# A GRU's first two steps: input products without Winograd sums, loads in order of use, ternary weights spread over VectorE

## The chip, the cores and the metric

The kernel runs on one core of a Trainium2 chip. The metric is device time in microseconds (us); for a kernel it is the median of several runs. TensorE (PE) multiplies, VectorE (DVE) and ScalarE (ACT) work on elements and read the products from PSUM, GpSimd (POOL) works on elements in SBUF and issues some DMAs, and SyncE (SP) issues most DMAs.

## The reference

Two blocks, each with a residual sum, on x of 128 sequences, 64 steps and 512 features, all in float32. Only the first concerns this change: a GRU over the 64 steps whose states go through a linear layer with ternary weights.

```python
def cell(h, x):
    gi = x @ W_ih + b_ih
    gh = h @ W_hh + b_hh
    i_r, i_z, i_n = jnp.split(gi, 3, axis=-1)
    h_r, h_z, h_n = jnp.split(gh, 3, axis=-1)
    r = jax.nn.sigmoid(i_r + h_r)
    z = jax.nn.sigmoid(i_z + h_z)
    n = jnp.tanh(i_n + r * h_n)
    h_new = (1.0 - z) * n + z * h
    return (h_new, h_new)
...
scale = jnp.mean(jnp.abs(weight))
w_t = jnp.clip(jnp.round(weight / (scale + EPS)), -1.0, 1.0)
w_ste = weight + jax.lax.stop_gradient(w_t * scale - weight)
return jnp.einsum('bsi,oi->bso', x, w_ste) + bias
```

The second block is a causal convolution over time, a mixture of 64 experts and a shared expert; the change leaves it as it is.

## The kernel before

The batch of 128 fills the partitions. A step t needs the input gates gi (x_t times W_ih, 512 by 1536) and the hidden gates (h times W_hh). The recurrence in h is serial: the hidden gates of step t are twelve 128x512 matmuls (L502), then come r, n, z and the new h on DVE and ACT (L509 to L523), then four transposes of h (L393) and a copy on ACT (L399).

The input gates don't depend on h, so they are made ahead and fill PE while the elementwise work of a step runs. They are made for two steps at a time: the pair of steps forms a 2 by 2 block matrix with the halves of the 512 features, W_ih of one gate a second one with the halves of its rows and columns. The two are multiplied by Winograd's form of Strassen's method: seven block products instead of eight, against sums of blocks. One product is two 128x256 matmuls (L338); the trace shows each float32 matmul as two passes, so a product is an entry "x4". `prepare(c)` makes the weight sums t1, t2, t4 and w12 of gate c on DVE (L287 to L292), and adds b_hh to b_ih where they can be added (L294). `pair_operands(t)` makes the sums of x: on POOL, for the first pair on DVE (L308 to L311). `Chunk.product(n)` makes product n and takes the results from PSUM on DVE, with the bias already in the chain (p1, u2, u3; L353 to L367).

`input_gates()` is a generator that gives one product at each `next`; the gates are taken in the order r, n, z, that is c = 0, 2, 1. Ahead of step 0 there are 24 products (20 of the first pair, which is all but its last, and four of the second pair in which that last one stands), and then 11 or 10 in each step: enough for a pair in two steps. In step 0's place in the order also lie the ternary weights: the load of wfT into xc0, the sum of its absolute values (L457, L460), a small matmul over the partitions (L462), the scale and the two bounds (L463 to L465), and for each of four parts of the weights two DVE instructions that make the signs `sgn` (L470, L471). The feed-forward product of step t - 1 (L417) is made in step t; its scale and residual are added on DVE (L428), with the bias fb added to x's rows on POOL ahead of it (L413).

The framework's scheduler orders each engine's instructions and sets the waits; `tc.issue_after(i)` puts what is made under it behind instruction i. Each tile pool has a number of buffers; a tile waits until the buffer's last reader is done. The PSUM tiles psx, psy, psw and psz have one buffer each.

The loads of the start go through SP's queue in program order: xp of the first pair, wih0 in two halves, biases, wih2, wih1, biases, h, xp of the second pair, whh0, whh2, whh1, fb, cb, rows of zeros, x's rows, wfT. From the ninth on, a DMA's issue waits until the eighth before it has landed.

Of the kernel before, what the change touches and what calls it, by code (L numbers as in the profile page):

```python
# [8 lines left out]
F32 = mybir.dt.float32  # L9
# [5 lines left out]
ALU = mybir.AluOpType  # L15
AX = mybir.AxisListType
# [3 lines left out]
P = 128  # L20
B = 128
T = 64
D = 512
KD = D // P
# [10 lines left out]
EPS = 1e-10  # L35
# [7 lines left out]
def adaln_ffn_kernel(  # L43
# [22 lines left out]
    nc = tc.nc  # L66
# [32 lines left out]
    def load_rows(dst, src):  # L99

        return nc.sync.dma_start(out=dst, in_=src.rearrange("(k p) n -> p k n", p=P))
# [98 lines left out]
    with (  # L200
# [11 lines left out]
        def load_pair(t, queue=nc.gpsimd):  # L212
            xp = xpp.tile([P, 2, KD, B], F32, name="xp")
            queue.dma_start(out=xp, in_=xT[t : t + 2].rearrange("t p k b -> p t k b"))
            xps[t] = xp
# [4 lines left out]
            (nc.sync if t < 3 else nc.gpsimd).dma_start(out=xn, in_=x[:, t, :])  # L220
            xns[t] = xn

        load_pair(0, nc.sync)
        h = el0.tile([P, D], F32, name="h")

        whh = [w0.tile([P, KD, D], F32, name=f"whh{c}") for c in range(3)]
# [12 lines left out]
        wi = wi_.enter_context(tc.tile_pool(name="wi", bufs=1))  # L239

        bi = wi.tile([P, 3 * D], F32, name="bi")
        wih = [wi.tile([P, KD, D], F32, name=f"wih{c}") for c in range(3)]

        xc0 = xcs[0].rearrange("p b e -> p (b e)")
        cols = [slice(c * D, (c + 1) * D) for c in range(3)]
# [1 line left out]
        def repeated(dst, row):  # L247
            nc.sync.dma_start(out=dst, in_=row.partition_broadcast(P))

        for h_ in range(2):
            half_ = slice(h_ * HD, (h_ + 1) * HD)
            load_rows(wih[0][:, h_ * HK : (h_ + 1) * HK], w_ih[half_, cols[0]])
        bh = {}
        for c in (0, 2, 1):
            if c:
                load_rows(wih[c], w_ih[:, cols[c]])
            repeated(bi[:, cols[c]], b_ih[cols[c]])
            if c != 2:  # L260
                bh[c] = el0.tile([P, D], F32, name="r")
                repeated(bh[c], b_hh[cols[c]])
        nc.sync.dma_start(out=h, in_=cond)
        load_pair(2, nc.sync)
        for c in (0, 2, 1):
            load_rows(whh[c], w_hh[:, cols[c]])
            if c == 0:
                repeated(bhn, b_hh[cols[2]])
        repeated(fb, fbias)
        repeated(cb, cbias)  # L270
        nc.gpsimd.memset(zrow, 0.0)
# [2 lines left out]

        nc.vector.memset(ones, 1.0)

        wsum = {}

        def prepare(c):

            w = wih[c]
            w11, w12 = w[:, :HK, :HD], w[:, :HK, HD:]
            w21, w22 = w[:, HK:, :HD], w[:, HK:, HD:]
            t1 = wi.tile([P, HK, HD], F32, name=f"t1{c}")
            nc.vector.tensor_sub(t1, w12, w11)  # L287
            t2 = wi.tile([P, HK, HD], F32, name=f"t2{c}")
            nc.vector.tensor_sub(t2, w22, t1)  # L289
            nc.vector.tensor_sub(w12, w22, w12)  # L290
            t4 = wi.tile([P, HK, HD], F32, name=f"t4{c}")
            nc.vector.tensor_sub(t4, w21, t2)  # L292
            if c in bh:
                nc.vector.tensor_add(bi[:, cols[c]], bi[:, cols[c]], bh[c])  # L294
            wsum[c] = {1: w11, 2: w21, 3: w22, 4: t4, 5: t1, 6: t2, 7: w12}

        gis, last = {}, []
        made = []

        def pair_operands(t):  # L300

            xp = xps.pop(t)
            x11, x12 = xp[:, 0, :HK], xp[:, 0, HK:]
            x21, x22 = xp[:, 1, :HK], xp[:, 1, HK:]
            s = xpp.tile([P, 3, HK, B], F32, name="xs")
            s1, s2, s4 = s[:, 0], s[:, 1], s[:, 2]
            engine = nc.gpsimd if t else nc.vector
            engine.tensor_add(s1, x21, x22)  # L308
            engine.tensor_sub(s2, s1, x11)
            engine.tensor_sub(x21, x11, x21)  # L310
            engine.tensor_sub(s4, x12, s2)  # L311
            return {1: x11, 2: x12, 3: s4, 4: x22, 5: s1, 6: s2, 7: x21}
# [56 lines left out]
        def input_gates():  # L369


            prev = None
            for t in range(0, T, 2):
                ops = pair_operands(t)
                for c in (0, 2, 1):
                    if t == 0:
                        prepare(c)
                    cur = Chunk(t, c, ops)
                    for n in (1, 6, 7, 3, 2, 4, 5):
                        which = prev if n == 3 else cur  # L380
                        if which:

                            with tc.issue_after(made[-1].ins) if t == 0 and made else nullcontext():
                                which.product(n)
                            yield
                    prev = cur
            prev.product(3)
            yield
# [7 lines left out]
        def transposed(src):  # L396
            ps = turned_up(src)
            hT = el0.tile([P, KD, B], F32, name="hT")
            nc.scalar.copy(hT, ps)  # L399
            return hT  # L400
# [6 lines left out]
            nc.vector.tensor_sub(lo, hT, hi)  # L407
            return hi, lo

        def ffn(t, pieces):  # L410

            xn = xns.pop(t)
            nc.gpsimd.tensor_add(xn, xn, fb)  # L413
            ps = ps_f.tile([P, D], F32, name="psf")
            for i, piece in enumerate(pieces):
                for k in range(KD):
                    nc.tensor.matmul(  # L417
                        ps,
                        piece[:, k, :],
                        sgn[:, k, :],  # L420
                        start=(i == 0 and k == 0),
                        stop=(i == 1 and k == KD - 1),
                    )
            if t < T - TAIL:
                x1 = io0.tile([P, D], F32, name="x1")
            else:
                x1 = last[0][:, t - (T - TAIL)]
            nc.vector.scalar_tensor_tensor(x1, ps, scale, xn, ALU.mult, ALU.add)  # L428
            if t < T - TAIL:
                nc.sync.dma_start(  # L430
                    out=x1c[:, T - 1 - t, :, :].rearrange("q b e -> b q e"),
                    in_=x1.rearrange("b (q e) -> b q e", e=DS),
                )
            if t == T - 1 - TAIL:
                for sl in range(2):
                    load_steps(sl, slice(0, LAST))
                for sl in range(2, NCB):
                    load_piece(sl)

            (nc.gpsimd if t >= T - TAIL else nc.sync).dma_start(out=out_t[t], in_=x1)  # L440
            if t == T - 1 - LAST:
                for sl in range(2):
                    load_toeplitz(sl)
                    load_steps(sl, slice(LAST, T))
# [3 lines left out]
        for _ in range(24):  # L448
            next(stream)
        hT = transposed(h)  # L450

        wf = xc0[:, : KD * D].rearrange("p (k o) -> p k o", k=KD)
        load_rows(wf, wfT)
        wfl = wf.rearrange("p k o -> p (k o)")
        nc.vector.tensor_reduce(  # L457
            part, wfl.rearrange("p (a c) -> p a c", a=T), AX.X, ALU.add, apply_absolute_value=True
        )
        nc.vector.tensor_reduce(total, part, AX.X, ALU.add)  # L460
        ps_s = ps_f.tile([P, D], F32, name="psf")
        nc.tensor.matmul(ps_s[:, 0:1], ones, total, start=True, stop=True)  # L462
        nc.vector.tensor_scalar(scale, ps_s[:, 0:1], 1.0 / (D * D), None, ALU.mult)  # L463
        nc.vector.tensor_scalar(half, scale, EPS, 0.5, ALU.add, ALU.mult)
        nc.vector.tensor_scalar(nhalf, half, -1.0, None, ALU.mult)  # L465


        for k in range(KD):
            neg = el0.tile([P, D], F32, name="r")
            nc.vector.tensor_scalar(neg, wf[:, k, :], nhalf, None, ALU.is_lt)  # L470
            nc.vector.scalar_tensor_tensor(sgn[:, k, :], wf[:, k, :], half, neg, ALU.is_gt, ALU.subtract)  # L471

        for t in range(T):
            if t + 1 < T:
# [31 lines left out]
            ps_r, ps_n, ps_z = ps_g  # L506

            r = el0.tile([P, D], F32, name="r")
            nc.vector.tensor_add(r, ps_r, gis.pop((t, 0)))  # L509
            nc.scalar.activation(r, r, AF.Sigmoid)  # L510
            n = el0.tile([P, D], F32, name="n")
            nc.vector.tensor_add(n, ps_n, bhn)  # L512
            nc.vector.tensor_mul(n, n, r)
# [9 lines left out]
            nc.vector.tensor_add(h_new, h_new, n)  # L523

            if t > 0:
                ffn(t - 1, pieces)
            for _ in range(11 - t % 2):
                next(stream, None)
            h = h_new
            if t < T - 1:  # L530
                hT = transposed(h)
# [231 lines left out]
    class Down:  # L763
# [37 lines left out]
        def block(self, name):  # L801

            if name == "v":
                self.accs["v"] = ps_y.tile([P, D], F32, name="y")[:, :QT]
            j, half_ = self.places[name]
            nc.tensor.matmul(
                self.accs[name],
                self.aT[:, full - 1, self.steps[j]],
                swd[:, full - 1, half_ * HD : (half_ + 1) * HD],
                start=(name == "v"),  # L810
                stop=False,
                skip_group_check=name != "v",
            )
# [707 lines left out]
```

## Time and profile before

| | us |
|---|---|
| median of 3 runs | 2654.07 |
| lowest and highest | 2651.58, 2656.09 |
| profiled execution | 2653.43 |
| its span | 2651.7 |
| first product (PE) | 6.24 |
| transposes of the first h (PE) | 32.07 |
| first hidden gates (PE) | 34.67 |
| wfT there, first reduce (DVE) | 36.55 |
| transposes of the new h of step 0 (PE) | 56.00 |

The times of the lower part are starts in the trace, counted from the start of the span. An entry of the timeline gives start, duration, engine, line, operation, output and inputs, shape and number of instructions; in brackets stands the engine's idle time before it and what ended it. A duration is that of the instruction from start to end; instructions of one engine overlap a little, so the distance from start to start is what one costs in a row of them.

### The profile page before, as it was taken

Reading aid. Unit: us, or ns where it says so; the run is one execution under the profiler, and the core shown is the slowest. Engines: PE = TensorE matmul, PEld = TensorE weight load, DVE = VectorE, ACT = ScalarE, POOL = GpSimd, SP = SyncE. Lnnn points to the kernel's source line nnn. Section 1 sums busy time; section 2 is a strip of 40 time slices with the busy share of each in tenths; the row PEclk is TensorE's granted clock in tenths of the full one; section 3 lists DMA queues with packets and bytes.
Section 4 is the critical chain, followed back from the end, with each engine's and each line's share of the span. In section 5 each row is a group of like instructions: output and inputs, shape, how many; then the busy total and the mean of one; then the engine's idle time right before and its main releaser. Section 6 shows DMA issues by size and latency. Waiting matters only on the chain.

```text
span 2651.7 us, 31084 instructions
## 1 busy us (share of the span) xinstructions
PE 2630.1 (99%) x11959; PEld 1818.1 (69%) x11959; DVE 1411.0 (53%) x3116; ACT 422.9 (16%) x779; POOL 458.6 (17%) x519
## 2 busy tenths in 40 slices
PE   8999999999999999999999999999999999999999
PEld 5666666666666666666668767888877666666667
DVE  6555555555555555555557755666674333434344
ACT  1111111111111111111110222222321111111111
POOL 2111121111111111111113100000002222222210
PEclk9999999999999999999999999999999999999999
DMA  5323232323322222322228921222256999998952
GB/s 195 70 56 61 53 63 55 67 56 62 61 49 52 44 52 44 76 44 52 44 56 279 337 52 22 43 64 64 76 157 180 286 314 285 292 328 261 303 176 48
DMA packets 475540, 323.33 MB, mean 122 GB/s; under 512 B 328960, under 2 KB 395136, under 8 KB 473216
## 3 DMA queue, kind: packets, MB, share of 16 engines
q1 hardware_dynamic: 446800, 248.18, 33.6%
q0 software_dynamic: 28592, 73.16, 11.3%
q8 instruction: 95, 1.56, 0.2%
q14 instruction: 53, 0.43, 0.0%
HBM read 235.01 MB, written 92.55 MB: 124 GB/s over the span
## 4 chain that ended last, share of the span: by engine, by line
PE 98%; DVE 1%; DMA 0%; issue 0%; ACT 0%; SPq 0%; DVEq 0%
PE psgh L502 25%; PE psz L695 7%; PE psw L695 7%; PE psx L695 7%; PE psw L338 6%; PE psz L338 6%; PE psx L338 6%; PE psf L417 4%; PE y L695 4%; PE py L1410 3%; PE psy L338 3%; PE pg L1384 3%; PE pu L1384 3%; PE y L870 2%; PE psc L182 2%; PE lg L1018 1%
## 5 line engine op out<-in xcount | busy, mean ns | idle before, releaser
L502 PE MATMUL psgh<-whh,hT 128*128 128x512 f32 x1536 | 674.7, 595 | 0.7 <-ACT hT L399 0.7
L502 PEld LDWEIGHTS psgh<-whh,hT 128*128 128x128 f32 x1536 | 286.6, 190 | 350.2 <-issue 336.3
L338 PE MATMUL psx<-wih,xp 128*128 128x256 f32 x768 | 198.7, 381 | 6.3 <-DMA wih<-in_w_ih_dram 6.2
L220 POOL DMA_DIRECT2D xn<-in_x_dram x61 | 34.0, 557 | 843.8 <-DVE x L428 832.2
L338 PEld LDWEIGHTS psx<-wih,xp 128*128 128x128 f32 x768 | 143.8, 191 | 25.9 <-issue 6.2
L512 DVE TENSOR_TENSOR n<-psgh,bhn 128x512 f32<-128x512 f32 x64 | 44.3, 692 | 175.6 <-PE psgh L502 175.6
L1393 DVE SCALAR_TENSOR_TENSOR a<-a,rw,pu 128x352 f32<-128x352 f32 x32 | 18.6, 581 | 220.4 <-PE pu L1384 220.4
L399 ACT COPY hT<-psf 128x512 f32<-128x512 f32 x64 | 37.5, 586 | 584.8 <-PE psf L393 584.8
L509 DVE TENSOR_TENSOR r<-psgh,gi 128x512 f32<-128x512 f32 x64 | 44.3, 691 | 139.8 <-PE psgh L502 139.8
L413 POOL TENSOR_TENSOR xn<-xn,fb 128x512 f32<-128x512 f32 x64 | 80.8, 1264 | 145.2 <-DMA xn<-in_x_dram 145.2
L972 POOL DMA_DIRECT2D out_dram<-hid x32 | 27.6, 1000 | 450.9 <-issue 332.9
L338 PE MATMUL psz<-wih,xs 128*128 128x256 f32 x384 | 98.7, 379 | 1.8 <-DVE gi L361 1.8
L338 PE MATMUL psy<-t,xs 128*128 128x256 f32 x384 | 99.9, 383 | 0.4 <-DVE t L289 0.4
L338 PE MATMUL psw<-wih,xp 128*128 128x256 f32 x384 | 99.4, 381 | 0.0
L338 PE MATMUL psw<-t,xp 128*128 128x256 f32 x384 | 98.8, 380 | 0.2 <-DVE u L359 0.2
L338 PE MATMUL psz<-t,xs 128*128 128x256 f32 x384 | 98.7, 379 | 0.0
L417 PE MATMUL psf<-sgn,hhi 128*128 128x512 f32 x256 | 95.4, 494 | 0.3 <-DVE hlo L407 0.3
L1410 PE MATMUL py<-wd,aeT 128*64 128x512 f32 (+1 forms) x384 | 89.5, 601 | 0.0
L353 DVE TENSOR_TENSOR p<-psx,bi 128x512 f32<-128x512 f32 x96 | 66.4, 692 | 37.6 <-PE psx L338 37.3
L515 ACT ACTIVATE n<-n 128x512 f32<-128x512 f32 x64 | 40.3, 629 | 274.0 <-DVE n L514 274.0
L695 PE MATMUL psx<-xr,swg 128*128 128x256 f32 x320 | 83.3, 383 | 0.0
L695 PE MATMUL psx<-hid,swg 128*128 128x256 f32 x320 | 82.4, 380 | 0.0
(311 smaller groups left out, 4711.6 us busy)
## 6 DMA issues: line engine op xcount, KB each, us to landing
wg<-in_w_gate_dram SPq DMA_DIRECT2D x64, 704.0 KB
wu<-in_w_up_dram SPq DMA_DIRECT2D x64, 704.0 KB
wd<-in_w_down_dram SPq DMA_DIRECT2D x64, 512.0 KB
x1c<-x SPq DMA_DIRECT2D x62, 256.0 KB
out_dram<-x SPq DMA_DIRECT2D x62, 256.0 KB
xn<-in_x_dram POOLq DMA_DIRECT2D x61, 256.0 KB, 4.1
xp<-in_xT_dram POOLq DMA_DIRECT2D x30, 512.0 KB, 5.0
xc<-x1c SPq DMA_DIRECT2D x28, 512.0 KB
```

The lines of the kernel that those rows point to most:

```text
L182: i = nc.tensor.matmul(ps[rows, j].rearrange("p h (u t) -> p h u t", u=2), xcs[sl % NCB][:, rows, g * 4 + j], tzs[sl % NCB][:, :, :, g * 4 ...
L338: i = nc.tensor.matmul(ps, self.ops[n][:, k, :], self.ws[n][:, k, :], start=(first and k == 0), stop=(k == HK - 1), skip_group_check=not f ...
L353: add(self.p1, both, b)
L413: nc.gpsimd.tensor_add(xn, xn, fb)
L417: nc.tensor.matmul(ps, piece[:, k, :], sgn[:, k, :], start=(i == 0 and k == 0), stop=(i == 1 and k == KD - 1),)
L502: nc.tensor.matmul(ps, hT[:, k, :], whh[c][:, k, :], start=(k == 0), stop=(k == KD - 1))
L509: nc.vector.tensor_add(r, ps_r, gis.pop((t, 0)))
L512: nc.vector.tensor_add(n, ps_n, bhn)
L695: i = nc.tensor.matmul(ps.rearrange("p (j b) -> p j b", b=P) if len(r.shape) == 3 else ps, lhs(k), r, start=(first and k == 0), stop=(k == ...
L870: nc.tensor.matmul(gu.rearrange("p (j b) -> p j b", b=P), swr[:, k].rearrange("p w n -> p (w n)"), rows[:, k], start=(k == 0), stop=(k == ...
L1384: nc.tensor.matmul(acc[halves[j]], self.xeT[:, k, halves[j]], self.ws[j][which][:, k, :], start=(k == 0), stop=(k == KD - 1),)
L1410: nc.tensor.matmul(py[halves[j]], self.aeT[:n, c, halves[j]], self.ws[j][2][:n, c, :], start=(c == 0), stop=(c == len(ech) - 1),)
```

## The change

- **First pair.** Steps 0 and 1 are no longer made by Winograd's form. `first_products(c, xp)` makes the eight plain block products of each gate, in an order in which each block of W_ih serves both steps one after the other, and ACT copies each finished 128x256 sum from PSUM into gi. This makes 24 products for the pair instead of 21. The biases are added to these gi later, on DVE (`first_biases`).
- **Sums.** `prepare` no longer comes ahead of each gate's products. Its DVE instructions and those of `first_biases` are chained by `in_order`, each behind the one before. `pair_operands` always uses POOL; the first pair has none.
- **Loads.** wih0 becomes four tiles of one block each, wih2 and wih1 two tiles of two blocks. SP's queue is in order of use: half of x's step 0, block (0,0), x's step 1, block (0,1), the other half of step 0, blocks (1,0) and (1,1), wih2, wih1, h, xp of the second pair, then biases and whh, and wfT right behind whh1, ahead of fb, cb and x's rows.
- **PE's start.** Seven 128x128 matmuls on the tile of ones, which nobody reads, precede the first product.
- **Ternary weights.** `ternary()` is a generator. The sum of absolute values becomes four instructions, each behind step 0's r on DVE; the scale follows; the four pairs of sign instructions come between the products of step 0, and what is left behind step 1's r. The temporary takes z's buffers instead of r's.
- **Feed-forward bias.** For t < 3, fb is added to x's rows on DVE, behind the r of the step, instead of on POOL.
- **Ahead of step 0**, after the transposes of h are put in, three products more are taken from the stream (27 in all).

```diff
-        load_pair(0, nc.sync)
+        xps[0] = xpp.tile([P, 2, KD, B], F32, name="xp")
...
-        for h_ in range(2):
-            half_ = slice(h_ * HD, (h_ + 1) * HD)
-            load_rows(wih[0][:, h_ * HK : (h_ + 1) * HK], w_ih[half_, cols[0]])
+        nc.sync.dma_start(out=xps[0][:, 0, :HK], in_=xT[0, :, :HK])
+        load_block(0, 0)
+        nc.sync.dma_start(out=xps[0][:, 1], in_=xT[1])
+        load_block(0, 1)
+        nc.sync.dma_start(out=xps[0][:, 0, HK:], in_=xT[0, :, HK:])
+        for n in range(2):
+            load_block(1, n)
+        for c in (2, 1):
+            for k in range(2):
+                load_half(c, k)
+        nc.sync.dma_start(out=h, in_=cond)
+        load_pair(2, nc.sync)
         bh = {}
         for c in (0, 2, 1):
-            if c:
-                load_rows(wih[c], w_ih[:, cols[c]])
             repeated(bi[:, cols[c]], b_ih[cols[c]])
             if c != 2:
                 bh[c] = el0.tile([P, D], F32, name="r")
                 repeated(bh[c], b_hh[cols[c]])
-        nc.sync.dma_start(out=h, in_=cond)
-        load_pair(2, nc.sync)
...
+        load_rows(whh[1], w_hh[:, cols[1]])
+        wf = xc0[:, : KD * D].rearrange("p (k o) -> p k o", k=KD)
+        load_rows(wf, wfT)
...
+        ps = ps_f.tile([P, D], F32, name="psf")
+        for _ in range(7):
+            nc.tensor.matmul(ps[:, :P], ones, ones, start=True, stop=True)
...
+        def first_biases(t):
+            for c in (0, 2, 1):
+                b = bi[:, cols[c]]
+                if t == 0 and c in bh:
+                    in_order(nc.vector.tensor_add, b, b, bh[c])
+                in_order(nc.vector.tensor_add, gis[t, c], gis[t, c], b)
+
+        def first_products(c, xp):
+            for t in range(2):
+                gis[t, c] = gip.tile([P, 2, HD], F32, name="gi").rearrange("p h d -> p (h d)")
+            accs = {}
+            for k in range(2):
+                for n in range(2):
+                    for t in range(2):
...
+                        for j in range(HK):
+                            i = nc.tensor.matmul(
+                                accs[t, n],
+                                xp[:, t, k * HK + j, :],
+                                block(c, k, n)[:, j, :],
+                                start=(k == 0 and j == 0),
+                                stop=(k == 1 and j == HK - 1),
+                            )
+                        made.append(i)
+                        if k == 1:
+                            nc.scalar.copy(gis[t, c][:, n * HD : (n + 1) * HD], accs[t, n])
+                        yield
...
-            for t in range(0, T, 2):
+            xp = xps.pop(0)
+            for c in (0, 2, 1):
+                for _ in first_products(c, xp):
+                    yield
+                if c == 0:
+                    prepare(0)
+            prepare(2)
+            first_biases(0)
+            prepare(1)
+            first_biases(1)
+            for t in range(2, T, 2):
...
-            nc.gpsimd.tensor_add(xn, xn, fb)
+            if t < 3:
+                with tc.issue_after(i.ins):
+                    nc.vector.tensor_add(xn, xn, fb)
+            else:
+                nc.gpsimd.tensor_add(xn, xn, fb)
...
+        for _ in range(3):
+            next(stream)
+        def ternary():
+            for k in range(KD):
+                with tc.issue_after(chain[-1].ins):
+                    nc.vector.tensor_reduce(
...
+            for k in range(KD):
+                yield
+                neg = el0.tile([P, D], F32, name="z")
+                nc.vector.tensor_scalar(neg, wf[:, k, :], nhalf, None, ALU.is_lt)
+                nc.vector.scalar_tensor_tensor(sgn[:, k, :], wf[:, k, :], half, neg, ALU.is_gt, ALU.subtract)
...
-            for _ in range(11 - t % 2):
+            for j in range(11 - t % 2):
                 next(stream, None)
+                if t == 0 and j in (0, 4, 8):
+                    next(signs)
```

## The prediction

> **What bounds the kernel now.** I read the page first (busy shares, then the chain that ended last), then busy time by stretches, then the timeline of the first 60 us. The page's busy line and its chain line:
>
> ```profile
> PE 2630.1 (99%) x11959; PEld 1818.1 (69%) x11959; DVE 1411.0 (53%) x3116; ACT 422.9 (16%) x779; POOL 458.6 (17%) x519
> ...
> PE 98%; DVE 1%; DMA 0%; issue 0%; ACT 0%; SPq 0%; DVEq 0%
> ```
>
> TensorE (PE) is the bound nearly everywhere, so the time is the PE's work plus the places where it stood still. Busy time by stretches says where those are (columns: stretch, its length, then busy us and instructions of each engine, clock, DMA share, GB/s):
>
> ```profile
> 0.00:60.00 60.00, 51.33 (x189) 35.89 (x190) 41.42 (x78) 6.22 (x8) 16.66 (x25) 1.00 0.62 215
> 60.00:800.00 740.00, 740.00 (x2655) 488.09 (x2654) 402.68 (x697) 105.66 (x171) 128.04 (x153) 1.00 0.30 58
> ```
>
> From 60 to 800 us PE has no gap at all; in the first 60 us it lacks 8.7 us. The change touches that start alone; the instructions of the rest stand in the same order, so whatever is won or lost there shifts all the rest by as much. The timeline, PE and DVE (start, length, engine, line, operands, count, idle before and who ended it):
>
> ```profile
> 6.24 2.04 PE L338 MATMUL psx<-wih,xp 128*128 128x256 f32 x4 [6.24 <-DMA wih<-in_w_ih_dram]
> 8.63 2.07 PE L338 MATMUL psy<-t,xs 128*128 128x256 f32 x4 [0.35 <-DVE t L289]
> 10.50 1.91 PE L338 MATMUL psw<-wih,xp 128*128 128x256 f32 x4
> 12.44 1.30 PE L338 MATMUL psx<-wih,xp 128*128 128x256 f32 x4
> ...
> 15.60 1.03 PE L338 MATMUL psx<-wih,xp 128*128 128x256 f32 x4
> 16.46 1.03 PE L338 MATMUL psy<-t,xs 128*128 128x256 f32 x4
> ```
>
> ```profile
> 36.55 2.29 DVE L457 TENSOR_REDUCE part<-xc 128x64 f32<-128x2048 f32 x1 [1.69 <-DMA xc<-in_wfT_dram]
> ...
> 44.94 1.41 DVE L471 SCALAR_TENSOR_TENSOR sgn<-xc,half,r 128x512 fp32r<-128x512 f32 x2
> ...
> 47.05 1.41 DVE L471 SCALAR_TENSOR_TENSOR sgn<-xc,half,r 128x512 fp32r<-128x512 f32 x2
> ...
> 48.38 0.68 DVE L509 TENSOR_TENSOR r<-psgh,gi 128x512 f32<-128x512 f32 x1
> ...
> 50.14 1.10 PE L338 MATMUL psz<-wih,xs 128*128 128x256 f32 x4 [1.76 <-DVE gi L361]
> ...
> 56.00 0.60 PE L393 MATMUL psf<-ident,h 128*128 128x128 f32 x4
> ```
>
> One block product (x4) starts every 0.865 us once warm (15.60, 16.46, 17.32), but the first three start about 2 us apart. The first waits until 6.24 for one megabyte of loads. Later the ternary work (the reduce waits for its weights, then eight sign instructions) sits on DVE ahead of r of step 0, which could have started near 38.4 (3.71 us after the gate products began at 34.67, as in step 1: 57.30 to 61.01) and starts at 48.38; PE then stands for 1.76 us at 50.14 and in pieces until 52.98.
>
> I take 56.00 as the mark: the transposes of h at the end of step 0. Work before it: 36 products x 0.865 = 31.14, transposes 0.44, gate products with the scale's small matmul 10.52 (34.67 to 45.19): 42.10. Elapsed from 6.24: 49.76. **Lost 7.66**: 4.17 in the first six products (6.24 to 15.60 against 6 x 0.865), 0.90 until 34.67, 2.59 from 45.19 to 56.00.
>
> **The Trainium skill.** "TensorE: Matmul & The Clock Gate", section "Part 1: The HAM clock gate", says that the array runs at half clock until a free-running window of about 3.4 us has been busy, so 3.4 to 6.8 us after the first matmul. The trace agrees in kind: products start 1.87 us apart while cold, and the fast rhythm begins near 12.4, 6.2 us after the first (with one gap of 0.35 in it). The same page's table of properties calls VectorE's queue strict FIFO: a waiting instruction holds all behind it, as L457 does above. "DMA: Bandwidth & Descriptors", section "Anatomy of one DMA", gives a fixed cost of some 2 us for a DMA of GpSimd's path; here, on SP's queue, the first load (0.5 MB) is issued at 0.81, and 3.25 us later, at 4.06, its reader starts. Its section "Why small descriptors are slow" counts 3 extra cycles a packet; for the 1 KB rows of the new blocks against 2 KB I estimate from it 35/32 against 67/64, some 4% more time. No run here shows that yet.
>
> **The change part by part.**
>
> *Earlier start.* Before, the first product needs 1.05 MB (xp and half of wih0). Now it needs 0.39 MB: half of x's first step and one block. In the trace data begins to move at about 2.0 us and flows at 296 GB/s in the stretch 2 to 4; 0.39 MB are in by 3.3, 3.5 with the smaller rows, and with 0.3 to 0.7 us to the semaphore (xp: 3.75 worked out, 4.06 seen) the product may start at 3.9 to 4.3. The seven matmuls on ones start at about 1.15 (the memset ends at 1.08); each is two passes of half the columns of L338's, so at the cold rate (1.73/8 = 0.215 a pass) they end near 4.15. Start: 4.2 instead of 6.24, **-2.04**. They cost nothing more, since PE would wait for the data; if the data came sooner they would hold it back by up to 0.3. The following loads keep ahead: 1.57 MB landed at 7.89 before and now serves eight products, which last until about 12.3.
>
> *Cold clock.* If PE is busy from 1.15, the clock should rise between 4.6 and 8.0; 6.2 us after the first, as before, gives 7.3. Half the time from 4.2 to there is lost: 0.2 to 1.9, I take **1.2**.
>
> *No sums before the first products.* The Winograd sums (L287 to L294) and the bias chain leave the path; each finished 128x256 sum is taken from PSUM by one ScalarE copy, 12 in all. The nearest row is a 128x512 ACT copy of 0.59, so about 0.4 each, against four products (3.46 us) between uses of a PSUM tile: hidden, ScalarE was idle until 32.7. Instead **three more products**: 24 for the first pair instead of 21, 3 x 0.865 = **+2.60**.
>
> *Order on DVE.* Sums for the later pairs and the adding of biases run behind. The last gate's bias add waits for ScalarE's copy after product 23 (25.9 by my schedule); behind it in the queue stand four sums, three adds, p1, u2, u3, eleven at 0.60 to 0.65, so free at 32.6, and r is due at 29.2 + 3.7 = 32.9. It fits with 0.3 to spare, while PE does the gate products (29.2 to 39.5) and needs none of it.
>
> *Ternary weights.* wfT moves ahead of the constants and of x's rows on SP's queue: 10.2 MB up to and with it. The stretches of the trace (6.1 MB by 20 us, 10.0 by 30) put it at 30.5 to 31.8, and 0.7 to 2.5 more to the semaphore. The four reduces (2.29/4 = 0.57 each) follow r at 33.5 and end at 35.9; n is due at 36.3. The four pairs of sign instructions (0.40 + 0.66) are spread over the eleven products of step 0. I laid DVE's queue out one by one: z 40.2, the new h 44.0, p1 44.6, then with two sign instructions between, u3 at 46.7, which PE's n = 4 product of that chunk wants at 46.6. So DVE is close to the limit there; **0.3** for gaps, 0 to 1.5 as bounds. The last signs end near 53.5; the first feed-forward product comes near 61. The add of fb to xn for three steps, now on DVE behind r (0.69 each), lies in an idle stretch: DVE waited 2.74 for psgh before n in step 1. POOL loses 3 x 1.24 us that nobody waited for. whh's loads, behind 5.0 MB, land by about 20.5, 25.2 and 28.6, needed at 29.2, 32.6 and 36.1.
>
> *Sum.* Start 4.2 + cold 1.2 + 24 products 20.76 + transposes 0.44 + 3 products 2.60 + gate products 10.3 + scale 0.24 + 11 products 9.52 + gaps 0.3 = 49.56 at the mark, against 56.00: -6.44. At the mark the new kernel has 637 of its 675 products to come, the old one 636 of 672: +0.87. Together **-5.6 us**. Cross-check: -2.04 - (7.66 - 1.5) + 2.60 = -5.6. On the profiled execution (2653.43; span 2651.7 and 1.7 around it) this is 2647.8; the median of the runs is 0.64 higher, so 2648.5.
>
> **Rivals.**
> 1. *Part of the gain is lost to late data or a late DVE.* If the start gets data at 300 GB/s less a quarter, or u3 and its followers are 1.5 us late, or the gate stays cold until near 9, the gain falls to about -2.5: 2651.6. For it: DVE's slack of 0.3 in two places, and DVE instructions that took 1.04 and 1.21 instead of 0.68 beside POOL (22.43, 23.40). Against: POOL's adds for pair 2 come before 20 us now, when DVE has room.
> 2. *Slower: wfT is late and takes the place of the old wait.* All of n, z, h and the evacuations stand behind the reduces in DVE's queue. PE loses what wfT lands after 33.9 (reduces 2.3, then the 10.4 from n to u3, against 46.6). Break-even is a landing at about 39.5; at 46 the loss is 12.1, the sum +6.5: 2660.6. For it: it landed at 36.55 before, 12.0 after its issue at 24.52. Against: it is now issued near 18 to 19, once the eighth load before it has landed, with 1.1 MB less ahead; the same flight gives 31.
>
> **How the numbers follow.** A difference under 0.2% (5.3 us) can hardly be told from none. Forecast 0.78, with its own range -7.8 to -3.6 (start 0.4, cold 0.7 to 1.0, gaps up to 1.2 either way); rival 1 0.15; rival 2 0.07. The forecast lies just beyond the bound; nearly three quarters of its chance (0.57) I put past it, because the page's clock window more often ends earlier than I took and the gaps may be none; the other 0.21 and rival 1 are "same", 0.36; rival 2 is "slower", 0.07. The range takes in rival 1: 2645.5 to 2652.8.
>
> **What would show it.** First product near 4.2, products 0.865 apart from about 7; step 0's gate products at about 29 instead of 34.67; no idle before them; reduces straight behind r without a wait for DMA; the transposes at about 49.6; from there every time about 5.6 earlier. Wrong would be: a reduce that waits for in_wfT, a PE gap over 1 us between 40 and 50, cold products past 9 us, or a different pace after 60 us.

## The result and the profile after

| | before | after |
|---|---|---|
| median of 18 runs, us | 2653.81 | 2648.81 |
| lowest and highest | 2651.58, 2656.09 | 2646.83, 2652.55 |
| profiled execution | 2653.43 | 2647.67 |
| its span | 2651.7 | 2645.9 |
| first product (PE) | 6.24 | 4.28 |
| first h's transposes (PE) | 32.07 | 26.28 |
| transposes of step 0's new h (PE) | 56.00 | 49.33 |
| transposes of step 1's new h (PE) | 76.43 | 70.62 |

The ratio of the times is 0.9981, with a 95% interval of 0.9975 to 0.9988: 5.0 us less (3.2 to 6.6). In the two profiled executions the span is 5.8 us shorter. The forecast was 2648.5. At 0.19% the gain stands just inside the 0.2% under which, the prediction says, a difference can hardly be told from none; its interval lies clear of zero.

First the page of the changed kernel, its busy line and its chain line:

```profile
PE 2631.8 (99%) x11985; PEld 1823.5 (69%) x11985; DVE 1402.9 (53%) x3103; ACT 427.4 (16%) x791; POOL 453.2 (17%) x516
...
PE 98%; DVE 1%; DMA 1%; issue 0%; SPq 0%; ACT 0%; DVEq 0%
```

PE is busy 1.7 us longer and still the bound: it makes three more products and the matmuls on ones, while fewer products run at half speed. Busy time by stretches of the changed kernel (stretch, length, busy us and instructions of PE, PEld, DVE, ACT and POOL, clock, DMA share, GB/s):

```profile
0.00:60.00 60.00, 58.87 (x226) 43.40 (x227) 37.66 (x66) 11.36 (x21) 13.59 (x22) 1.00 0.61 215
60.00:800.00 740.00, 740.00 (x2657) 488.69 (x2656) 402.69 (x701) 105.87 (x171) 127.05 (x153) 1.00 0.30 58
```

In the first 60 us PE is busy 58.87 us, against 51.33 before; from 60 to 800 us it is busy throughout, as before. The clock column reads 1.00 although the first products run at half speed; that is seen from the distances between their starts. The timeline of the changed kernel's start, on PE:

```profile
1.13 3.36 PE L303 MATMUL psf<-ones 128*128 128x128 f32 x14 [1.13 <-DVE ones L299]
4.28 1.97 PE L345 MATMUL psx<-wih,xp 128*128 128x256 f32 x4
6.05 1.41 PE L345 MATMUL psw<-wih,xp 128*128 128x256 f32 x4
7.29 1.03 PE L345 MATMUL psy<-wih,xp 128*128 128x256 f32 x4
8.15 1.03 PE L345 MATMUL psz<-wih,xp 128*128 128x256 f32 x4
...
26.28 0.60 PE L461 MATMUL psf<-ident,h 128*128 128x128 f32 x4
...
29.31 10.46 PE L583 MATMUL psgh<-whh,hT 128*128 128x512 f32 x24
...
46.74 1.03 PE L399 MATMUL psw<-t,xp 128*128 128x256 f32 x4
...
49.33 0.60 PE L461 MATMUL psf<-ident,h 128*128 128x128 f32 x4
```

No entry from the first product on has a bracket, so PE waits for nothing that the profile shows. The distances from start to start of the first products are 1.77, 1.24 and 0.86: the clock is released (goes from half to full speed) about 6.8 us after the start of the span, in the middle of the second product. The same stretch on DVE:

```profile
6.94 0.69 DVE L323 TENSOR_TENSOR t<-wih,wih 128x512 f32<-128x512 f32 x1 [5.87 <-DMA wih<-in_w_ih_dram]
...
32.95 0.69 DVE L590 TENSOR_TENSOR r<-psgh,gi 128x512 f32<-128x512 f32 x1
33.87 2.47 DVE L532 TENSOR_REDUCE part<-xc 128x16 f32<-128x512 f32 x4 [0.23 <-DMA xc<-in_wfT_dram]
...
37.17 0.69 DVE L603 TENSOR_TENSOR n<-n,r 128x512 f32<-128x512 f32 x1
37.90 0.69 DVE L604 TENSOR_TENSOR n<-n,gi 128x512 f32<-128x512 f32 x1
...
45.95 0.41 DVE L420 TENSOR_TENSOR u<-psw,u 128x256 f32<-128x256 f32 x1
```

The gate r of step 0 starts 3.64 us after its products, at 32.95 instead of 48.38; the reduces follow it at once, save for 0.23 us in which they wait for the weights. The last line, u3, ends at 46.36 and with it frees the PSUM tile psw, into which the product at 46.74 writes: DVE is in time by 0.38 us. The first line waits for block (0,1) of wih0, which the third product (7.29) needs too; the block is there only 0.35 us before that product starts.

Where the 5.8 us come from, from the two traces. The first product starts 1.96 earlier. The first six products lose 1.28 instead of 4.17 (8.15 against 4.28 + 3 x 0.865, and none after it): 2.89. The idle 0.90 us before the first gate products and the 2.59 us in step 0 are gone. Three products more cost 2.60. Sum: -1.96 - 2.89 - 0.90 - 2.59 + 2.60 = -5.74. At the mark, the transposes of step 0, the difference is -6.67, and the one product that is made later brings it back by 0.87 to -5.80. From the transposes of step 1 to the end of the span it is 2575.3 us in both. So close an agreement is partly luck: in the other executions below this stretch is 2575.1 us (e8) to 2580.3 us (e10) long (see the last section).

### The profile page after: what moved, and what is told of

The parts are those of the page before. It is cut to its first block, busy times and chain, and to the rows that moved or that the text cites. A ratio compares the mean times of both kernels' runs of the same rounds, so it can differ in the third digit from the quotient of the medians.

```text
span 2645.9 us, 31136 instructions
## 1 busy us (share of the span) xinstructions
PE 2631.8 (99%) x11985; PEld 1823.5 (69%) x11985; DVE 1402.9 (53%) x3103; ACT 427.4 (16%) x791; POOL 453.2 (17%) x516
## 4 chain that ended last, share of the span: by engine, by line
PE 98%; DVE 1%; DMA 1%; issue 0%; SPq 0%; ACT 0%; DVEq 0%
PE psgh L583 25%; PE psz L787 7%; PE psw L787 7%; PE psx L787 7%; PE psz L399 6%; PE psw L399 6%; PE psx L399 6%; PE psf L490 4%; PE y L787 4%; PE py L1502 3%; PE psy L399 3%; PE pg L1476 3%; PE pu L1476 3%; PE y L962 2%; PE psc L182 2%; PE psf L461 1%
## 5 line engine op out<-in xcount | busy, mean ns | idle before, releaser
L399 PE MATMUL psx<-wih,xp 128*128 128x256 f32 x744 | 191.0, 379 | 0.0
```

The source lines that it names most:

```text
L399: i = nc.tensor.matmul(ps, self.ops[n][:, k, :], self.ws[n][:, k, :], start=(first and k == 0), stop=(k == HK - 1), skip_group_check=not f ...
```

## The experiments

The release of the clock isn't at the same time in each execution, so profiles of the same start differ: with the seven matmuls on ones and the plain first products the fourth product starts between 6.84 (e9) and 8.35 (e8). So I read two marks: the start of the fourth product, and the distance d from it to the transposes of step 1's new h, in which the release no longer plays a part. It is 62.47 in three executions (after, e1, e8). Medians are of several runs; the ratio is to the kernel before, run on the same chip.

| run | median, us | ratio and 95% interval | 4th product | step 1's transposes | d |
|---|---|---|---|---|---|
| after | 2648.81 | 0.9981 (0.9975 to 0.9988) | 8.15 | 70.62 | 62.47 |
| e1, no warm-up | 2650.35 | 0.9986 (0.9979 to 0.9993) | 9.04 | 71.51 | 62.47 |
| e2, warm-up doubled | 2650.23 | 0.9985 (0.9979 to 0.9992) | 8.38 | 71.01 | 62.63 |
| e3, wfT late | 2650.16 | 0.9984 (0.9977 to 0.9990) | 8.04 | 71.23 | 63.19 |
| e4, ternary before r | 2651.54 | 0.9989 (0.9981 to 0.9998) | 8.34 | 72.59 | 64.25 |
| e5, before with warm-up | 2654.06 | 1.0001 (0.9992 to 1.0009) | 12.35 | 76.49 | |
| e6, Winograd for the first pair | 2653.04 | 0.9997 (0.9988 to 1.0005) | 12.98 | 74.75 | |
| e7, fb's add on POOL | 2651.53 | 0.9992 (0.9985 to 0.9999) | 8.09 | 71.52 | 63.43 |
| e8, the changed kernel again | 2649.49 | 0.9984 (0.9976 to 0.9992) | 8.35 | 70.82 | 62.47 |
| e9, fb's add on POOL, behind r | 2648.45 | 0.9978 (0.9969 to 0.9988) | 6.84 | 69.71 | 62.87 |
| e10, Winograd for two gates | 2649.19 | 0.9980 (0.9971 to 0.9989) | 7.03 | 69.75 | 62.72 |

My theory: the gain is the sum of the early data, the plain products that need no sums, and the ternary weights out of r's way; the warm-up matters little. The rivals: that the clock alone did it (e1, e2, e5), that the order of the loads did it and the plain products only cost (e6, e10), that the move of the ternary work gives nothing (e3, e4), and that moving fb's add matters after all (e7, e9).

**The clock: e1, e2, e5.** e1 takes the matmuls on ones out of the changed kernel:

```
-        ps = ps_f.tile([P, D], F32, name="psf")
-        for _ in range(7):
-            nc.tensor.matmul(ps[:, :P], ones, ones, start=True, stop=True)
```

> The changed kernel without the seven matmuls on ones. Cold-clock theory (the dummies start the clock's release early): first product still near 4.2, products 1.8 us apart until 8 to 11 instead of until about 6.8, mark (transposes of step 0's new h) at 50.8 instead of 49.33, time +1.5 (+0.4 to +2.1) on the changed kernel. Rival (the release comes at a fixed time whatever PE does, or the dummies only delay the data's first use): mark 49.2 to 49.3, time 0 to -0.1.

e2 doubles them:

```
-        for _ in range(7):
+        for _ in range(14):
```

> Fourteen matmuls on ones instead of seven. Theory: they end near 7.3 (28 passes, 0.24 us each until the release near 6.8, then 0.11), the first product starts there warm, against 4.28 and 1.28 lost to the cold clock with seven: mark +1.8, time +1.8. If dummies were free as long as they end before the release, the time would stay as it is.

e5 puts eleven of them into the kernel before:

```
+        ps = ps_f.tile([P, D], F32, name="psf")
+        for _ in range(11):
+            nc.tensor.matmul(ps[:, :P], ones, ones, start=True, stop=True)
```

> The kernel before with eleven matmuls on ones ahead of its first product, nothing else. Theory (in the old order the first products wait for more than the clock: sums wait for the second half of wih0, and the bias b_hh lands near 10.9, so p1 and the fourth product cannot start before 12.4): first product near 6.5, warm; fourth product still near 12.4; time 0 to -0.5 on the kernel before. Rival (the cold clock made the loss of 4.17 in the first six products): about -1.7 to -3.

The timeline of e1 on PE, its first and its fourth product:

```profile
4.14 2.05 PE L342 MATMUL psx<-wih,xp 128*128 128x256 f32 x4 [4.14 <-DMA wih<-in_w_ih_dram]
...
9.04 1.03 PE L342 MATMUL psz<-wih,xp 128*128 128x256 f32 x4
```

Without the warm-up the data are there at 4.14, so the ones held nothing back by more than 0.14. The products start at 4.14, 5.98, 7.68 and 9.04: two at half speed, and a third that loses 0.50 of its 0.865, so the clock is released near 8.7 here. The fourth product starts 0.89 later than after, and d is the same to the hundredth: all of e1's loss is at the start. The runs alone don't separate e1 from after (the intervals overlap). The timeline of e2 on PE:

```profile
1.13 4.82 PE L303 MATMUL psf<-ones 128*128 128x128 f32 x28 [1.13 <-DVE ones L299]
5.79 1.03 PE L345 MATMUL psx<-wih,xp 128*128 128x256 f32 x4
```

The 28 passes would take 6.0 us cold, at 0.215 each; they took 4.82, so the clock was released in this execution near 4.4 (by this sum after 15 slow passes, with 13 fast ones behind them), and the first product, late at 5.79, was already at full clock. What the longer warm-up delays it gives back in faster products, and step 1's transposes are only 0.39 later than after, where I had expected far more. That was a miss: I had taken the release, near 6.8, as given. The timeline of e5 on PE:

```profile
6.10 1.18 PE L342 MATMUL psx<-wih,xp 128*128 128x256 f32 x4
8.61 1.13 PE L342 MATMUL psy<-t,xs 128*128 128x256 f32 x4 [1.32 <-DVE t L293]
...
12.35 1.13 PE L342 MATMUL psx<-wih,xp 128*128 128x256 f32 x4 [1.75 <-DVE p L357]
```

The products of the old start are fast now (1.18 instead of 2.04), and PE waits that much longer for the weight sums on DVE and for the bias in p. Step 1's transposes are at 76.49, against 76.43. So the slow clock alone was not what held the old start: behind it stood the loads and DVE's sums. The rival falls.

**The plain products: e6, e10.** e6 keeps the new order of blocks and the warm-up, but makes the first pair with Winograd's seven products; biases are loaded between the weights.

```
-            for c in (0, 2, 1):
-                for _ in first_products(c, xp):
-                    yield
...
-            for t in range(2, T, 2):
+            for t in range(0, T, 2):
                 ops = pair_operands(t)
                 for c in (0, 2, 1):
+                    if t == 0:
+                        prepare(c)
```

> The changed kernel with the first pair by Winograd's form again (21 products, sums and biases ahead of them, biases loaded among the weights as before the change); loads by blocks, the seven matmuls and the spread ternary work stay. Theory (plain products are what lets the start go ahead without sums and biases): first product near 4.3, but the fourth still waits for p1 and so for the biases, near 12; six products end near 15.5; time about +3.0 on the changed kernel, so -2 to -3 on the one before. Rival (early blocks alone make the gain at the start, and the three products more only cost): -2.6 on the changed kernel.

The timeline of e6 on PE:

```profile
4.28 2.05 PE L400 MATMUL psx<-wih,xp 128*128 128x256 f32 x4
9.06 2.08 PE L400 MATMUL psy<-t,xs 128*128 128x256 f32 x4 [2.73 <-DVE t L313]
10.93 1.91 PE L400 MATMUL psw<-wih,xp 128*128 128x256 f32 x4
12.98 1.68 PE L400 MATMUL psx<-wih,xp 128*128 128x256 f32 x4
15.50 1.13 PE L400 MATMUL psw<-t,xp 128*128 128x256 f32 x4 [0.85 <-DVE u L421]
...
17.33 1.03 PE L400 MATMUL psx<-wih,xp 128*128 128x256 f32 x4
...
32.87 0.60 PE L454 MATMUL psf<-ident,h 128*128 128x128 f32 x4
```

The first product starts as early as in the changed kernel, but the second needs all four blocks and a sum; PE stands for 2.73 us, and products are slow until near 14. This start is slower than expected (the seventh product starts at 17.33, and not near 15.5) and slower than the old one: the first h's transposes come at 32.87, 0.80 later than before the change. Step 1's transposes are at 74.75, 1.68 earlier than before, but that comes from step 0: from the first transposes to those of step 1 it is 41.88 us instead of 44.36, and there the ternary work and fb's add are as in the changed kernel. So the early blocks alone keep nothing of the gain at the start, and the second rival falls. With three products (2.60) less to do, e6 is still 4.13 later than after: the plain products are dearer by 2.60 and save 6.7. Part of the 6.7 is the clock, which stays slow until near 14 after PE has stood still; what e6 would lose with a fast clock isn't shown.

e10 asks for the middle: plain products for gate r alone, Winograd for n and z. Two products fewer than after, 1.73 us, could be won.

```
-            for c in (0, 2, 1):
-                for _ in first_products(c, xp):
-                    yield
+            for _ in first_products(0, xp):
+                yield
...
+                for c in (0, 2, 1) if t else (2, 1):
```

> The changed kernel with plain products for gate r of the first pair only; n and z by Winograd's form, whose sums DVE has time for by then; their biases are loaded between the weights, wfT ahead of the last part of whh. Two products fewer. Theory: no new wait, transposes of step 1's h at 68.9 instead of 70.62, time -1.7 on the changed kernel, so about -6.7 on the one before. Rival (a bias or sum arrives late as in the full Winograd start, or wfT is late for the earlier r): 69.8 to 71, time -0.8 to +0.4 on the changed kernel.

The timeline of e10 on PE, the two places where it stood longest:

```profile
16.08 1.13 PE L406 MATMUL psw<-t,xp 128*128 128x256 f32 x4 [1.00 <-DVE u L427]
...
23.06 1.13 PE L406 MATMUL psw<-t,xp 128*128 128x256 f32 x4 [0.34 <-DVE u L427]
```

The saving would have made d 62.47 - 1.73 = 60.74; it is 62.72. The 1.98 us went into waits for DVE, which has the sums and biases of two gates to do while products come every 0.865 us. This is what the rival expected. The median, 2649.19, can't be told from after's: two products fewer gain nothing here.

**The ternary weights: e3, e4.** e4 puts the ternary work back ahead of r of step 0:

```
-                with tc.issue_after(chain[-1].ins):
-                    nc.vector.tensor_reduce(
+                nc.vector.tensor_reduce(
...
+        for _ in ternary():
+            pass
         for t in range(T):
...
-            if t == 0:
-                signs = ternary()
-                next(signs)
```

> The ternary work as before the change, whole and ahead of r of step 0 on DVE (the load stays early). Theory (the block of eight sign instructions on DVE made the 2.59 us of gaps): r starts near 42.5 instead of 32.95, PE gaps of 1.5 to 2.5 in all between 43 and 50, mark with one product fewer before it near 50.8, time +2.4 on the changed kernel (+1.5 to +3.5). If the early load of wfT alone had removed the gaps: 0 to +0.5.

e3 leaves it behind r and loads wfT later, behind fb, cb, the zeros and x's first row, with n of step 0 held behind the reduces:

```
-        load_rows(wf, wfT)
         repeated(fb, fbias)
...
         load_x(0)
+        load_rows(wf, wfT)
...
+            with tc.issue_after(reduced[-1].ins) if t == 0 else nullcontext():
+                nc.vector.tensor_add(n, ps_n, bhn)
```

> wfT's load goes back behind fb, cb, the zero rows and x's first rows, as before the change; n of step 0 stays behind the reduces on DVE. Theory (second rival of the prediction: what lands late is lost from about 34.3 on): landing near 36, reduces wait about 2.5 for DMA, PE gaps between 42 and 49, mark +1.5 to +2.5, time the same. If DVE has more room than I counted: 0 to +0.5.

The timeline of e4, two lines of PE and between them one of DVE:

```profile
7.37 1.13 PE L345 MATMUL psy<-wih,xp 128*128 128x256 f32 x4 [1.05 <-DMA wih<-in_w_ih_dram]
...
43.21 0.68 DVE L591 TENSOR_TENSOR r<-psgh,gi 128x512 f32<-128x512 f32 x1
...
44.88 1.13 PE L399 MATMUL psx<-wih,xp 128*128 128x256 f32 x4 [1.24 <-DVE gi L424]
```

r comes 10.3 us later than after, PE stands for 1.24 us at 44.88 and shorter at other places, and d grows by 1.78. The loss has the same form as before the change (1.76 us at 50.14 there). Most of the idle 2.59 us of the old step 0 is thus the ternary work ahead of r. (The first line lies ahead of the fourth product, so it is not in d; it is taken up again below.) The timeline of e3 on DVE:

```profile
36.70 2.47 DVE L534 TENSOR_REDUCE part<-xc 128x16 f32<-128x512 f32 x4 [3.17 <-DMA xc<-in_wfT_dram]
```

The weights are there 2.8 us later than after, and the reduce waits 3.17 us; d grows by 0.72 only. This was a miss: I had put the price near the delay itself. The orders on DVE and PE also moved with the edit, so the run doesn't say what a late load costs in the order of the changed kernel, only that most of 2.8 us can be absorbed.

**fb's add: e7, e9.** e7 leaves the add of fb to x's rows on POOL, as before the change.

```
-            if t < 3:
-
-                with tc.issue_after(i.ins):
-                    nc.vector.tensor_add(xn, xn, fb)
-            else:
-                nc.gpsimd.tensor_add(xn, xn, fb)
+            nc.gpsimd.tensor_add(xn, xn, fb)
```

> The bias fb is added to x's rows on POOL for all steps, as before the change. Theory (the adds lie in idle stretches on either engine): mark and time as the changed kernel, within 0.3. If it mattered that DVE does them: over 0.5 either way.

The timeline of e7, in order of time, POOL, DVE and PE:

```profile
33.49 2.46 DVE L527 TENSOR_REDUCE part<-xc 128x16 f32<-128x512 f32 x4
33.76 0.72 POOL L369 TENSOR_TENSOR xs<-xp 128x256 f32<-128x256 f32 x1 [6.12 <-DMA xp<-in_xT_dram]
...
36.61 4.62 POOL L481 TENSOR_TENSOR xn<-xn,fb 128x512 f32<-128x512 f32 x3
...
37.11 1.31 DVE L598 TENSOR_TENSOR n<-n,r 128x512 f32<-128x512 f32 x1
38.46 1.64 DVE L599 TENSOR_TENSOR n<-n,gi 128x512 f32<-128x512 f32 x1
40.79 0.98 DVE L606 TENSOR_TENSOR h<-h,n 128x512 f32<-128x512 f32 x1 [0.70 <-ACT n L600]
...
42.76 1.13 PE L399 MATMUL psx<-wih,xp 128*128 128x256 f32 x4 [0.24 <-DVE gi L424]
```

Another miss, and the most useful one. Nothing waits for the three adds in this stretch, and yet d grows by 0.96. They lie beside n and h, and these three instructions take 1.31, 1.64 and 0.98 us where after's take 0.69 each: 1.86 us more on an engine that had 0.38 to spare, of which 0.96 reached PE. The adds themselves take 1.54 each instead of 1.24. "SBUF: two separate sides", a section of the Trainium skill's page "SBUF — State Buffer", says that VectorE and GpSimd share a pair of ports under an exclusive lock: of a VectorE operation with two SBUF inputs and a GpSimd operation that reads SBUF, the one that "starts first gets the pair for the whole instruction; the other fully blocks". The trace agrees. Taken one by one, the adds run from 36.61 to 37.87, from 37.84 to 39.55 and from 39.51 to 41.23; n, n and h end at 38.42, 40.10 and 41.77, each 0.54 to 0.55 after the end of an add. So the engines take turns. It agrees too where no lock is due: the reduces have one input and take 2.46 us beside POOL's sums at 0.72. Before the change the adds lay elsewhere, POOL and DVE:

```profile
39.16 3.72 POOL L413 TENSOR_TENSOR xn<-xn,fb 128x512 f32<-128x512 f32 x3
...
41.73 0.69 DVE L512 TENSOR_TENSOR n<-psgh,bhn 128x512 f32<-128x512 f32 x1 [2.90 <-PE psgh L502]
```

DVE stood still until 41.73, and the n that follows, beside the last add, has one input from PSUM and takes its usual 0.69.

e9 tests this: the adds are on POOL again, but behind a small copy of r of the step in which they are made, away from n of step 0.

```
+                first = nc.gpsimd.tensor_copy(late, r[:, :1])
+                with tc.issue_after(first.ins):
+                    nc.gpsimd.tensor_add(xn, xn, fb)
```

> The adds of fb on POOL for the first three steps, but each held back until the r of the step that uses it (by a one-column copy of r on POOL ahead of it), so that they no longer run beside n of step 0. Theory (two elementwise streams, on POOL and DVE, slow each other; the 0.90 of the last experiment came from 1.31, 1.64 and 0.98 for n, n and h beside POOL's adds): n and n take 0.69 again, transposes of step 1's h at 70.6 to 70.8, the 0.90 is gone. Rival (an add on POOL costs as such, or the loss came from another order on DVE): it stays at 71.5.

The timeline of e9, two lines of DVE and one of POOL:

```profile
33.98 2.46 DVE L533 TENSOR_REDUCE part<-xc 128x16 f32<-128x512 f32 x4 [1.45 <-DMA xc<-in_wfT_dram]
...
37.15 0.69 DVE L604 TENSOR_TENSOR n<-n,r 128x512 f32<-128x512 f32 x1
37.88 0.69 DVE L605 TENSOR_TENSOR n<-n,gi 128x512 f32<-128x512 f32 x1
...
54.98 1.26 POOL L485 TENSOR_TENSOR xn<-xn,fb 128x512 f32<-128x512 f32 x1
```

The two n take 0.69 again. Step 1's transposes, at 69.71, lie below the 70.6 to 70.8 expected, because the first product already runs at full clock in this execution; d is 62.87, 0.40 over after's; of that 0.21 lies before 25.18, in the products ahead of step 0, 0.17 from there to step 0's transposes, where the wait for wfT grew to 1.45 as all before it was 1.1 us earlier in this execution, and 0.02 in all that comes later. So it isn't the engine that counts but what lies beside it. The median, 2648.45, can't be told from after's.

**The changed kernel again: e8**, without any edit, beside e9 and e10.

> The changed kernel once more, beside the next two. Transposes of step 1's h at 70.62 as before, within 0.4 (the cold clock's release moves); time 5.0 under the kernel before, 3.5 to 6.5.

d is 62.47 again, and the span 2645.9. The fourth product starts 0.20 later, within the 0.4 expected.

## Why the prediction was right, and where not

*Start* (4.2 predicted): 4.28. Without the ones the first product starts at 4.14 (e1), as worked out, so they hold back next to nothing. "The following loads keep ahead" holds less firmly: in e4, whose clock was released near 4.6, the third product waited 1.05 us for block (0,1), while e9 and e10, released just as early, show no such wait.

*Cold clock* (1.2, bounds 0.2 to 1.9): 1.28, the size right in part by luck. Read from the first products, the release came near 4.2 (e9), 4.4 (e2), 4.6 (e4), 6.8 (after) and, without the warm-up, 8.7 (e1). So "6.2 us after the first, as before" isn't a property of the kernel, and two of these lie ahead of the earliest time that the prediction allowed, 4.6. Nor is the 1.28 all the clock's: block (0,1) was there only 0.35 us before the third product, so by estimate an earlier release could have saved about 0.35 in that execution. The skill's page named in the prediction says in the same section that the window is free-running and that the ramp is "run-variable"; the traces agree. What the warm-up is worth stays open: the fourth product starts at 6.84 to 8.35 with it and at 9.04 in the one profile without, 0.7 to 2.2 us later, and the medians don't separate the two.

*No sums before the first products; three more products* (2.60): right. e6 shows that the early blocks gain nothing at the start without products that need nothing but blocks. e5 shows that the clock would have gained nothing by itself. No run has the plain products with the old order of loads, or without the three taken ahead of step 0, so these shares aren't shown.

*Order on DVE, ternary weights* (gaps 0.3; mark 49.56): no gap, mark at 49.33. The prediction had the weights there at 31 to 34 and no wait in front of the reduces; they were there at 33.87, at the late end, and the reduces waited 0.23, which cost nothing. By the prediction's own list a reduce that waits for in_wfT was a sign of being wrong; here it was too short to be one. It had u3 as the narrow place, and u3 is in time by 0.38. e4 puts the worth of moving this work out of r's way at 1.8 us, for the reduces and the sign instructions together. The second rival, a late wfT, did not come; its price, "PE loses what wfT lands after 33.9", is called into question by e3, which lost 0.72 for 2.8 us.

*The step that failed: fb's add.* The prediction costed it at nothing: "lies in an idle stretch", and "POOL loses 3 x 1.24 us that nobody waited for". Both are true of the profile before, where the adds ran from 39.16, for the most part beside a DVE that stood still. In the new order they would have run at 36.6, beside n, and e7 shows that keeping them there costs 0.96 us. So this edit guards a sixth of the gain, and is not housekeeping; by e9, adds on POOL at a later place would have done as well. The sign of it was in the prediction's own text: DVE instructions "that took 1.04 and 1.21 instead of 0.68 beside POOL", listed as a risk and not turned into a price for these adds. The sum came out all the same, because it was made with durations of an undisturbed DVE, and these the edit brings about.

*The sum* (-5.6 on the execution, 2648.5 for the median): -5.8 in the profiles, -5.0 between the medians. The interval of the runs, 3.2 to 6.6, holds both. That the profiles meet the forecast to 0.2 us is partly luck: the cold clock took from nothing (e9) to 1.5 us (e8) of the same start, and the stretch behind the edit varies by more than a microsecond between executions. The stated range, 2645.5 to 2652.8, begins lower than its own terms give: 7.8 under the median of 2654.07 is 2646.3. What I put too high was the chance of more than 0.2%: a forecast of 5.6 us against a bound of 5.3 left no room for that.

## What to carry to other kernels

At a start that waits for data, look for products that need only what has landed, even where they are more in number: three more products of 0.865 us saved 6.7 us of waiting and of slow products here (e6 against after), while a warmer clock alone bought nothing (e5). Before an instruction is called hidden because nobody waits for it, look at what lies beside it in the new order, not in the old: a GpSimd add beside a VectorE operation with two SBUF inputs made the latter up to 2.4 times as long. And where starts of single executions differ, measure from a mark behind the disturbance to one behind the edit.

## What was not expected of the hardware

The two engines slow each other at other places too. The timeline of the changed kernel from 15 us on, in order of time, DVE and POOL:

```profile
16.19 1.21 POOL L369 TENSOR_TENSOR xs<-xp 128x256 f32<-128x256 f32 x1 [10.23 <-DMA xp<-in_xT_dram]
16.73 1.22 DVE L323 TENSOR_TENSOR t<-wih,t 128x512 f32<-128x512 f32 x1
...
33.81 0.72 POOL L369 TENSOR_TENSOR xs<-xp 128x256 f32<-128x256 f32 x1 [6.11 <-DMA xp<-in_xT_dram]
```

The same sum on POOL takes 1.21 us beside DVE's sums of two SBUF inputs and 0.72 beside the reduces of one.

A second thing stays open. At the end of the GRU, near 1385 us, PE stands still twice, for 1.65 and 0.68 us in e8 and for 1.66 and 0.68 us in e9, and in some executions the granted clock falls there. The stretch of e8 and that of e9, in columns as above:

```profile
1385.00:1390.00 5.00, 2.88 (x9) 1.48 (x10) 2.08 (x4) 1.20 (x2) 0.00 (x0) 1.00 0.55 74
```

```profile
1385.00:1390.00 5.00, 3.84 (x8) 1.93 (x9) 1.12 (x2) 1.20 (x2) 0.00 (x0) 0.66 0.64 107
```

e8 keeps 1.00; e9 has 0.66, by estimate 0.34 x 5 = 1.7 us of full clock. The gate products there take 11.57 us to the next start instead of 10.00. In e3, e4, e7 and e10 there is such a drop too (0.91 over 1380 to 1400, as in e9), in before, after, e1, e2, e5 and e6 there is none (1.00). It may be part of why medians differ by more than the marks do (e7: 2.7 us over after, with 0.96 in d). The stretch from step 1's transposes to the end is 2575.1 to 2576.6 us long without a drop and 2576.7 to 2580.3 with one, so the drop isn't all. The skill's page on the clock gate ("Part 1: The HAM clock gate") has the clock fall after an idle window of about 3.4 us; here no gap is that long, the same gaps go with and without a drop, and what decides it stays open.
